# A four-layer transformer issued in turns, in the order of its source

## The chip, the cores and the metric

The kernel runs on one core of one Trainium2 chip. The metric is the device time of one execution in microseconds. A core has five engines with a queue each: TensorE (PE, with its weight loads shown apart as PEld), VectorE (DVE), ScalarE (ACT), GpSimd (POOL) and SyncE (SP), which here issues the DMAs. Each engine takes its instructions in the order in which they stand in its queue, and waits where one needs a result of another engine.

## The reference

A tensor of 16 sequences of 256 tokens with 128 features goes through eight blocks, each added to the residual stream after a layer norm on either side. The third block, the one that is touched here, is itself a transformer of four layers:

```python
for i in range(DEPTH):      # 4
    x = x + self_attention(layer_norm(x, ln1_g[i], ln1_b[i]), Wq[i], Wk[i], Wv[i], Wo[i], bo[i])
    h = layer_norm(x, ln2_g[i], ln2_b[i])
    x = x + (jax.nn.gelu(h @ W1[i] + b1[i], approximate=False) @ W2[i] + b2[i])
```

Its self-attention has eight heads of 16. Four are local: windows of 128 tokens, where a query sees its own window up to itself and the window before it. Four are linear: a softmax over the features of q, elu(k) + 1, and a context per 64 tokens that is summed over the earlier ones. The MLP is 128 to 512 to 128 with a Gelu. All numbers are float32.

## The kernel before

The 16 sequences are handled as eight groups (`NG`) of two sequences, 512 tokens each, in four tiles of 128 tokens (`NT`). The whole program is one stage after another; each stage has its own pools of SBUF and PSUM. `stage_l1_attn` (L761) is the stage of the four-layer transformer. Its input is `z[g]`, the normed residual stream of group g, and it keeps the stream of the four layers in `z[g]`.

A group's layer has two generators. `l1_mix` (L832) is the attention: norm and transposes (`l1_norm_T`, L806), the products for Q and K (L848, L852), a product for the token-major rest (L864) with maxima and copies on DVE and ACT, then for each of two sequences the scores of the local heads with a mask added by a product (L883 to L890) and their row maxima on DVE (L891). The maxima are transposed onto Q (`q2T`, L905), the scores are computed a second time transposed (L933, L935), exponentiated on ACT (L938), cut to the causal part on POOL (L941), and multiplied with the values (L950, L952) into one PSUM tile with the tag `o`. The linear heads' context (L920) and products (L960) run beside. Two rounds of transposes (L975, L981) lead to the output product (L985), which DVE adds to `z` (L986). `l1_ffn` (L815) is the MLP: norm and transposes, four first products with a Gelu each (L824), the second products (`tokens_ps`, L338) into one PSUM tile, and an add on DVE (L829). A statistic of a norm is four instructions L255 and four L257 on DVE, then L244 and L245 on POOL; the norm itself is four L264 on DVE.

PSUM has eight banks. In this stage seven of them are one ring for the tags `s`, `mm` and `t`, and one is `o` (`RING_BANKS`, L37). All products go through the helper at L336, all transposes of a norm through L325, so the profile names products by their tiles. A float32 product appears as two passes in the profile: two MATMUL and two LDWEIGHTS.

What sets the order: the stage is traced by `interleave` (L219), which advances up to five generators at a time, one `yield` each in a round. The list has, for every layer, eight mixes and then eight MLPs. But the stage isn't in a manual schedule, so this is no more than a preference: the planner of the tile framework orders the instructions of each engine by its own costs and by what it takes to be ready. Other stages (`stage_l0`, the attentions, the last one) stand in `k.tc.manual_schedule()`, where every engine has its instructions in the order in which the source traces them, by the helper `turns`:

```python
def turns(self, items):
    now = 0
    items = [[start, 0, steps] for start, steps in items]
    while items:
        for item in items[:]:
            for _ in range(min(3, now - item[0] + 1 - item[1])):
                item[1] += 1
                if next(item[2], self) is self:
                    items.remove(item)
                    break
        now += 1
```

In each turn every item that has started takes one step, from one `yield` to the next, in the order of the list. `idle(n)` is n empty steps.

The stage before (`stage_l0`) leaves the last group's first MLP output, `y7`, unfinished; `rest_of_l0` (L752) norms and adds it beside the first mix. In the last layer `ffn` (L782) also norms and adds the result to `x[g]` for groups 0 to 5, and `then` (`fill`, L994) stores `x[g]` and norms it for the next stage. Groups 6 and 7 (`k.over`) leave that to the next stage, which can't start before this one has given back its pools.

Of the kernel before, what the change touches and what calls it, by code (L numbers as in the profile page):

```python
# [750 lines left out]

def rest_of_l0(k, x, z, y):  # L752

    yield from k.residual(x, y)
    yield
    nb, rs = k.stats_nb(x)
    yield
    k.normed_act(z, x, nb, rs)


def stage_l1_attn(k, x, ws, rows, z, then, xn, y7, xT0):  # L761


    nc = k.nc

    k.l1_val = [k.t([P, NT, 4, 32], f"l1_val{i}", 1) for i in range(3)]
    k.l1_lin = [k.t([P, NT, 65], f"l1_lin{i}", 1) for i in range(3)]
    k.l1_ctx = [k.t([P, 4, 68], f"l1_ctx{i}", 1) for i in range(2)]  # L770
    k.l1_max = [k.t([P, 2, 3, 4, 32], f"l1_max{i}", 1) for i in range(2)]
    for a in k.l1_val + k.l1_lin:
        nc.vector.memset(a, 1.0)
    for a in k.l1_max + k.l1_ctx:
        nc.gpsimd.memset(a, 0.0)
    for a in k.l1_ctx:
        nc.gpsimd.tensor_copy(a[:, :, 64:68], bc(k.c["head16"], 1, 4))
    k.cb = {n: k.t([P, P], "b_" + n, 1, dt=BF16) for n in ("ident", "negmask")}
    for n, a in k.cb.items():
        nc.vector.tensor_copy(a, k.c[n])  # L780

    def ffn(i, g):  # L782
        late = i == 3 and g in k.over
        yield from l1_ffn(k, z[g], ws[i], rows[f"b2{i}"], xn[g] if late else z[g])
        if i == 3 and not late:
            yield
            yield from k.residual(x[g], z[g])
            yield
            yield from then(g)

    steps, leads = [], []
    for i in range(4):
        steps += [l1_mix(k, z[g], ws[i], rows[f"bo{i}"], NG * i + g, xT0 if i + g == 0 else None) for g in range(NG)]
        steps += [ffn(i, g) for g in range(NG)]
        leads += [4] * NG + [2] * NG

    def beside(a, b):
        for _ in a:
            next(b, k)
            yield  # L800

    steps[0] = beside(steps[0], rest_of_l0(k, x[NG - 1], z[NG - 1], y7))
    k.interleave(steps, 5, leads, -1)


def l1_norm_T(k, z, g, b):  # L806

    xn = yield from k.norm(z, "xn")
    ps = k.transposed_ps(xn)
    out = k.t([P, GT], "xT", 2)  # L810
    k.nc.scalar.activation(out, ps, AF.Identity, bias=b, scale=g)
    return out


def l1_ffn(k, z, w, b2, out):  # L815

    hT = yield from l1_norm_T(k, z, w["ln2_g"], w["ln2_b"])
    k.nc.gpsimd.tensor_tensor(z, z, bc(b2, 1, NT), ALU.add)
    yield
    h = k.t([P, 4, GT], "mlp_h", 3)  # L820
    for f in range(4):
        ps = k.ps("s")
        k.mm(ps, w["w1"][:, f * P : (f + 1) * P], hT)
        k.nc.scalar.activation(h[:, f, :], ps, AF.Gelu, bias=w["b1"][:, f : f + 1])  # L824
        if f % 2:
            yield
    ps = k.tokens_ps(h, w["w2"].rearrange("p (c n) -> p c n", c=4))
    yield
    k.nc.vector.tensor_tensor(out, ps, z, ALU.add)  # L829


def l1_mix(k, z, w, bo, n, hT=None):  # L832
# [6 lines left out]
    heads = [slice(32 * h, 32 * h + 32) for h in range(4)]  # L839
    tiles = lambda b: [slice((2 * b + t) * P, (2 * b + t + 1) * P) for t in range(2)]  # L840
    if hT is None:
        hT = yield from l1_norm_T(k, z, w["ln1_g"], w["ln1_b"])
    nc.gpsimd.tensor_tensor(z, z, bc(bo, 1, NT), ALU.add)
    yield

# [6 lines left out]
    k.mm(ps, w["wk"], hT)  # L852
    kT = k.t([P, GT], "kT", 3)
    nc.scalar.activation(kT, ps, AF.Identity, bias=k.c["one16"])

    q = k.t([P, 2, 2, 64], "q", 2)
    kr = k.t([P, NT, 64], "kr", 2)
# [2 lines left out]
    for half in range(2):  # L860
# [10 lines left out]
        nc.scalar.activation(ke[:, ts, :], ps[:, :, 64:128], AF.Exp)  # L871
        nc.scalar.copy(val[:, ts, :, 0:16], ps[:, :, 128:192].rearrange("p t (h d) -> p t h d", d=16))
        nc.scalar.copy(lin[:, ts, 0:64], ps[:, :, 192:256])
    yield

# [3 lines left out]
    for b in range(2):  # L879
        (q0, q1), both = tiles(b), slice(2 * b * P, (2 * b + 2) * P)  # L880
        ss = [k.ps("s") for _ in heads]
        for r, s in zip(heads, ss, strict=True):
            k.mm(s[:, 0:P], qT[r, q0], kT[r, q0], True, False)  # L883
        for r, s in zip(heads, ss, strict=True):
            k.mm(s[:, P : 3 * P], qT[r, q1], kT[r, both], False, False)


        for h, s in enumerate(ss):
            s = s[:, : 3 * P].rearrange("p (j n) -> p j n", j=3)
            k.mm(s[:, 0:3:2, :], ident, bc(negmask, 1, 2), False, True)  # L890
            v.tensor_reduce(mx[:, b, :, h, 16], s, AX.X, ALU.max, negate=True)  # L891
        v.tensor_tensor(mx[:, b, 1, :, 16], mx[:, b, 1, :, 16], mx[:, b, 2, :, 16], ALU.min)
        if b == 0:


            nc.scalar.activation(q, q, AF.Exp)
            v.scalar_tensor_tensor(ke, ke, 1.0, kr, ALU.min, ALU.add)
        yield
    q2T = k.t([P, GT], "q2T", 2)
    tp = k.ps("mm")  # L900
    for b in range(2):
        for t in range(2):
            at = mx[:, b, t].rearrange("p h n -> p (h n)")
            nc.tensor.transpose(tp[:, (2 * b + t) * P : (2 * b + t + 1) * P], at, k.c["ident"])
    v.tensor_tensor(q2T, tp, qT, ALU.add)  # L905

    halves = [slice(0, 64), slice(64, P)]
    tp = k.ps("mm")
# [1 line left out]
        nc.tensor.transpose(tp[:, t * P : (t + 1) * P], q[:, t].rearrange("p b n -> p (b n)"), k.c["ident"])  # L910
    linT = k.t([P, SEQ], "linT", 2)
    nc.scalar.copy(linT, tp[:, :SEQ])

    cps = k.ps("mm")[:, : 3 * 65].rearrange("p (u n) -> p u n", u=3)
    first = slice(0, 64)
# [13 lines left out]
    for b in range(2):  # L929
        (q0, q1), both = tiles(b), slice(2 * b * P, (2 * b + 2) * P)  # L930
        ss = [k.ps("s") for _ in heads]
        for r, s in zip(heads, ss, strict=True):
            k.mm(s[:, 0:SEQ], kT[r, q0], q2T[r, both], True, False)  # L933
        for r, s in zip(heads, ss, strict=True):
            k.mm(s[:, SEQ : 3 * P], kT[r, q1], q2T[r, q1], False, True)  # L935
        e = k.t([P, 4, 3, P], "e", 3)
        for h, s in enumerate(ss):
            nc.scalar.activation(e[:, h].rearrange("p j n -> p (j n)"), s[:, : 3 * P], AF.Exp)  # L938
# [50 lines left out]
def soft_inputs(k, x, pool):  # L989
# [1 line left out]
    xs = k.dram.tile([P, NG, NT, D], F32, tag="xs", name="xs")  # L991
    xn = [pool.tile([P, NT, D], F32, tag=f"mxn{g}", name=f"mxn{g}") for g in range(NG)]

    def fill(g):  # L994
        k.nc.sync.dma_start(out=xs[:, g], in_=x[g])
        nb, rs = k.stats_nb(x[g])
        yield
        k.normed_act(xn[g], x[g], nb, rs)

    return xs, xn, fill  # L1000
# [1067 lines left out]
```

## Time and profile before

| | |
|---|---|
| median of 3 runs | 2963.91 us (2961.12 to 2964.82) |
| profiled execution, its own time | 2960.44 us |
| its span, from the first to the last instruction | 2958.7 us |
| mean granted TensorE clock | 0.968 of full |
| PE busy | 2757.9 us, 93% of the span |
| DVE, ACT, POOL busy | 1931.3, 1676.9, 1017.2 us |
| the changed stage | from 175.0 to 948.45 us |

The profile shows one execution. A group of instructions is given by source line, engine, operation and tiles (written, then read), with a count, the busy time and the mean length; after a bar stand the idle time of the engine ahead of them and who ended it. A timeline line gives start, length, engine, line, operation, tiles, shape and count, and in brackets the idle time before it and what released it. The ends of matmuls are modelled and they overlap in the pipeline, so a stretch of TensorE is best read from start to start.

### The profile page before, as it was taken

What the parts mean: (1) busy time and instruction counts of PE and PEld (TensorE: products, weight loads), DVE (VectorE), ACT (ScalarE), POOL (GpSimd) and SP (SyncE); (2) the same over time, 40 slices, a digit from 0 to 9 for tenths busy, and PEclk for the clock granted to TensorE, in tenths of its full rate; (3) what the DMA queues carried; (4) which work ended last, traced back from release to release, by engine and by line L of the source; (5) the groups of instructions that cost most, each with busy time, mean ns of one, the idle gap of its engine ahead of it and who ended that gap; (6) DMA issues with size and microseconds to landing.
All of it is one profiled execution on the core that took longest, in us unless ns stands there. A gap on an engine that the chain in (4) does not pass through costs nothing.

```text
span 2958.7 us, 59454 instructions
## 1 busy us (share of the span) xinstructions
PE 2757.9 (93%) x23674; PEld 1878.8 (63%) x23674; DVE 1931.3 (65%) x5302; ACT 1676.9 (57%) x3530; POOL 1017.2 (34%) x1407
## 2 busy tenths in 40 slices
PE   8989999999998799999988998799999799978998
PEld 4556776777766588888863443566666444436897
DVE  5677466565666889999967765666574587735442
ACT  6745656455465676777735666444434377756543
POOL 3553333333336200000044555423221466644332
PEclk9989999999999899999988999899999899998999
DMA  4000000000001000000020000000000000010000
GB/s 116 12 1 2 1 2 2 1 2 1 2 2 38 1 12 12 8 9 8 9 71 5 1 1 1 1 1 1 1 1 1 1 1 1 1 51 7 2 16 16
DMA packets 29150, 31.30 MB, mean 11 GB/s; under 512 B 7292, under 2 KB 20156, under 8 KB 28732
## 3 DMA queue, kind: packets, MB, share of 16 engines
q1 hardware_dynamic: 28872, 27.49, 3.1%
q8 instruction: 187, 3.06, 0.4%
q14 instruction: 91, 0.75, 0.1%
HBM read 23.29 MB, written 4.19 MB: 9 GB/s over the span
## 4 chain that ended last, share of the span: by engine, by line
PE 50%; ACT 7%; DVE 7%; POOL 2%; issue 2%; DMA 0%; POOLq 0%; SPq 0%; ACTq 0%; DVEq 0%
PE ps_s L336 31%; PE ps_o L336 7%; PE ps_mm L336 6%; ACT at_e L491 1%; PE ps_s L325 1%; ACT lg L1199 1%; PE ps_xin L336 1%; ACT meT L1206 1%; PE ps_sum L336 1%; ACT mdisp L1106 1%; ACT lg L1079 1%; PE ps_t L1204 1%; DVE at_nm L459 1%; PE ps_s L525 1%; DVE scan L1488 1%
## 5 line engine op out<-in xcount | busy, mean ns | idle before, releaser
L459 DVE TENSOR_REDUCE at_nm<-ps_s 128x2 f32<-128x512 f32 (+1 forms) x384 | 238.1, 682 | 119.7 <-PE ps_s L336 119.7
L491 ACT ACTIVATE at_e<-ps_s 128x512 f32<-128x512 f32 x384 | 198.2, 603 | 96.7 <-PE ps_s L336 94.6
L1488 DVE TENSOR_TENSOR scan<-ps_s,lm 128x384 f32<-128x384 f32 x256 | 124.7, 549 | 142.4 <-PE ps_s L336 142.2
L497 POOL TENSOR_SCALAR_AFFINE_SELECT at_e<-at_e 128x1024 f32<-128x1024 f32 (+1 forms) x96 | 135.1, 1408 | 208.1 <-ACT at_e L491 207.8
L245 POOL TENSOR_TENSOR ln_rs<-ln_rs,mhalf 128x4 f32<-128x4 f32 x192 | 196.6, 1024 | 15.2
L1015 POOL TENSOR_TENSOR ln_rs<-ln_mv,mendt 128x4 f32<-128x4 f32 x6 | 1.2, 199 | 521.2 <-DVE ln_mv L1013 521.2
L891 DVE TENSOR_REDUCE l_max<-ps_s 128x3 f32<-128x384 f32 x256 | 124.1, 548 | 61.5 <-PE ps_s L336 61.5
L336 PE MATMUL ps_o<-my,meT 128*128 128x129 f32 x1024 | 144.1, 288 | 20.8 <-ACT mgot L1218 16.5
L336 PEld LDWEIGHTS ps_s<-l_w,mlp_h 128*128 128x128 f32 x1280 | 149.7, 192 | 20.3 <-issue 15.1
L336 PE MATMUL ps_s<-l1f_phi,mxT 128*128 128x256 f32 x512 | 141.8, 401 | 21.5 <-DVE mpart L1080 15.7
L244 POOL TENSOR_SCALAR ln_rs<-ln_mv 128x4 f32<-128x4 f32 x184 | 38.5, 209 | 338.0 <-DVE ln_mv L257 317.3
L336 PEld LDWEIGHTS ps_o<-my,meT 128*128 128x128 f32 x1024 | 127.8, 195 | 39.3 <-ACT mgot L1218 22.2
L336 PE MATMUL ps_s<-l_w,mlp_h 128*128 128x128 f32 x1280 | 151.0, 275 | 1.3 <-ACT mlp_h L824 0.9
L336 PE MATMUL ps_s<-qm,kT 32*128 32x512 f32 x768 | 144.4, 650 | 8.0 <-DVE at_nm L459 7.8
L336 PE MATMUL ps_s<-km,qT 32*128 32x512 f32 x768 | 138.4, 666 | 8.7 <-DVE qT L1632 3.7
L941 POOL TENSOR_SCALAR_AFFINE_SELECT e<-e 128x512 f32<-128x512 f32 x128 | 78.6, 635 | 172.8 <-ACT e L938 172.8
L336 PE MATMUL ps_o<-at_e,at_vm 128*32 128x128 f32 (+1 forms) x2048 | 122.7, 336 | 15.3 <-ACT at_oT L521 15.3
L336 PE MATMUL ps_mm<-mdisp,mxn 128*128 128x128 f32 x1024 | 125.3, 279 | 5.0 <-DVE mdisp L1118 4.9
L938 ACT ACTIVATE e<-ps_s 128x384 f32<-128x384 f32 x256 | 105.4, 510 | 39.4 <-PE ps_s L336 39.4
L1465 ACT COPY BT<-ps_s 128x512 f32<-128x512 f32 x64 | 37.6, 587 | 158.0 <-PE ps_s L336 158.0
L336 PEld LDWEIGHTS ps_mm<-mdisp,mxn 128*128 128x128 f32 x1024 | 121.8, 195 | 7.9 <-DVE mdisp L1118 6.6
L336 PEld LDWEIGHTS <-b_ident 128*128 128x128 bf16 x656 | 51.9, 99 | 113.1 <-issue 102.5
(462 smaller groups left out, 7203.1 us busy)
## 6 DMA issues: line engine op xcount, KB each, us to landing
mw<-in_l1fw SPq DMA_DIRECT2D x16, 256.0 KB, 2.6
moe_w<-in_moe SPq DMA_DIRECT2D x16, 256.0 KB, 5.4
l_w<-in_l SPq DMA_DIRECT2D x10, 256.0 KB, 3.3
x<-in_x SPq DMA_DIRECT2D x8, 256.0 KB, 5.8
xs<-x SPq DMA_DIRECT2D x8, 256.0 KB, 2.1
out<-x SPq DMA_DIRECT2D x8, 256.0 KB, 2.5
slT<-xs SPq DMA_DIRECT2D x6, 256.0 KB, 2.7
l1f_phi<-in_l1f SPq DMA_DIRECT2D x1, 1024.0 KB, 5.0
```

Source lines behind the costliest of these rows:

```text
L244: g.tensor_scalar(out, in_, scale, eps, ALU.mult, ALU.add)
L245: g.tensor_tensor(out, out, self.mhalf[:, :n], ALU.pow)
L325: self.nc.tensor.transpose(out[:n, k * P : (k + 1) * P], src[:, k, cols], self.c["ident"])
L336: self.nc.tensor.matmul(out, lhsT=lhsT, rhs=rhs, start=start, stop=stop, skip_group_check=True)
L459: v_.tensor_reduce(nm[:, t, r, vs], s, AX.X, ALU.max, negate=True)
L491: nc.scalar.activation(e[:, r], s, AF.Exp)
L497: nc.gpsimd.affine_select(at, at, [[0, 4], [0, n], [1, P]], ALU.is_ge, 0.0, base=0, channel_multiplier=-1)
L891: v.tensor_reduce(mx[:, b, :, h, 16], s, AX.X, ALU.max, negate=True)
L938: nc.scalar.activation(e[:, h].rearrange("p j n -> p (j n)"), s[:, : 3 * P], AF.Exp)
L941: nc.gpsimd.affine_select(e[:, :, j, :], e[:, :, j, :], [[0, 4], [1, P]], ALU.is_ge, 0.0, base=0, channel_multiplier=-1)
L1465: nc.scalar.copy(s, ps)
L1488: v.tensor_tensor(m, s[:, : SEQ + P], lm[:, SCAN_HEADS[4 * (t // 2) + 2 * i + hh], :], ALU.mult)
```

## The change

The stage gets a manual schedule. Each mix and each MLP is an item of `turns`. Mix n (layer n // 8, group n % 8) has its transposes in turn `at[n]`: 0, 5, 11, 16, 22 and from then on every eight turns. Its norm begins six turns earlier, its last step is 16 turns later, and the MLP of the same group and layer begins 17 turns after `at[n]`. The items stand in the list by falling start, so within a turn the item that started last comes first. `rest_of_l0` is the last item and starts at turn 0.

For this the steps are cut anew. A mix has yields between Q, K and the first half of the values, between the halves, two after the first sequence's scores, one after Q's exponential, one ahead of the linear context, an empty one between the sequences' second scores, one between the two weighted sums and one behind their copy. Norms wait 5 steps in a mix, 3 in an MLP, and there is one more step between a norm and its transposes. The exponential of `q` stands behind both sequences' scores instead of the first's, the sum for `ke` behind `q2T`.

Two things change in the work itself. The masks are the first product into each score tile instead of the last; the maxima then follow the scores directly. And an MLP's second products go into the `o` tile instead of one of the ring, in three parts (tile 0; tiles 1 and 2; tile 3) with a step each. `mlp_h` has two buffers instead of three. The numbers computed are the same.

```diff
 def rest_of_l0(k, x, z, y):
-    yield from k.residual(x, y)
+    yield from k.residual(x, y, 3)
     yield
     nb, rs = k.stats_nb(x)
-    yield
+    yield from idle(3)
     k.normed_act(z, x, nb, rs)
...
         if i == 3 and not late:
             yield
-            yield from k.residual(x[g], z[g])
+            yield from k.residual(x[g], z[g], 3)
             yield
-            yield from then(g)
-    steps, leads = [], []
-    for i in range(4):
-        steps += [l1_mix(k, z[g], ws[i], rows[f"bo{i}"], NG * i + g, xT0 if i + g == 0 else None) for g in range(NG)]
-        steps += [ffn(i, g) for g in range(NG)]
-        leads += [4] * NG + [2] * NG
...
-    steps[0] = beside(steps[0], rest_of_l0(k, x[NG - 1], z[NG - 1], y7))
-    k.interleave(steps, 5, leads, -1)
+            yield from then(g, 3)
+    at = [0, 5, 11, 16, 22] + [32 + 8 * n for n in range(4 * NG - 5)]
+    items = []
+    for n, start in enumerate(at):
+        i, g = divmod(n, NG)
+        items.append((start - (0 if n == 0 else 6), l1_mix(k, z[g], ws[i], rows[f"bo{i}"], n, xT0 if n == 0 else None)))
+        items.append((start + 17, ffn(i, g)))
+    items = sorted(items, key=lambda item: -item[0])
+    with k.tc.manual_schedule():
+        k.turns(items + [(0, rest_of_l0(k, x[NG - 1], z[NG - 1], y7))])
-def l1_norm_T(k, z, g, b):
-    xn = yield from k.norm(z, "xn")
+def l1_norm_T(k, z, g, b, wait):
+    xn = yield from k.norm(z, "xn", 2, wait)
+    yield
     ps = k.transposed_ps(xn)
...
 def l1_ffn(k, z, w, b2, out):
-    hT = yield from l1_norm_T(k, z, w["ln2_g"], w["ln2_b"])
+    hT = yield from l1_norm_T(k, z, w["ln2_g"], w["ln2_b"], 3)
...
-    h = k.t([P, 4, GT], "mlp_h", 3)
+    h = k.t([P, 4, GT], "mlp_h", 2)
...
-    ps = k.tokens_ps(h, w["w2"].rearrange("p (c n) -> p c n", c=4))
-    yield
+    ps = k.ps("o").rearrange("p (t d) -> p t d", t=NT)
+    w2 = w["w2"].rearrange("p (c n) -> p c n", c=4)
+    for t in range(NT):
+        for f in range(4):
+            k.mm(ps[:, t, :], h[:, f, t * P : (t + 1) * P], w2[:, f, :], f == 0, f == 3)
+        if t in (0, 2):
+            yield
     k.nc.vector.tensor_tensor(out, ps, z, ALU.add)
...
-        hT = yield from l1_norm_T(k, z, w["ln1_g"], w["ln1_b"])
+        hT = yield from l1_norm_T(k, z, w["ln1_g"], w["ln1_b"], 5)
...
     nc.scalar.activation(kT, ps, AF.Identity, bias=k.c["one16"])
+    yield
...
         nc.scalar.copy(lin[:, ts, 0:64], ps[:, :, 192:256])
-    yield
+        if half == 0:
+            yield
...
         ss = [k.ps("s") for _ in heads]
+        for s in ss:
+            k.mm(s[:, : 3 * P].rearrange("p (j n) -> p j n", j=3)[:, 0:3:2, :], ident, bc(negmask, 1, 2), True, False)
         for r, s in zip(heads, ss, strict=True):
-            k.mm(s[:, 0:P], qT[r, q0], kT[r, q0], True, False)
+            k.mm(s[:, 0:P], qT[r, q0], kT[r, q0], False, False)
         for r, s in zip(heads, ss, strict=True):
-            k.mm(s[:, P : 3 * P], qT[r, q1], kT[r, both], False, False)
+            k.mm(s[:, P : 3 * P], qT[r, q1], kT[r, both], False, True)
         for h, s in enumerate(ss):
             s = s[:, : 3 * P].rearrange("p (j n) -> p j n", j=3)
-            k.mm(s[:, 0:3:2, :], ident, bc(negmask, 1, 2), False, True)
             v.tensor_reduce(mx[:, b, :, h, 16], s, AX.X, ALU.max, negate=True)
         v.tensor_tensor(mx[:, b, 1, :, 16], mx[:, b, 1, :, 16], mx[:, b, 2, :, 16], ALU.min)
         if b == 0:
-            nc.scalar.activation(q, q, AF.Exp)
-            v.scalar_tensor_tensor(ke, ke, 1.0, kr, ALU.min, ALU.add)
-        yield
+            yield
+            yield
+    nc.scalar.activation(q, q, AF.Exp)
+    yield
...
     v.tensor_tensor(q2T, tp, qT, ALU.add)
+    v.scalar_tensor_tensor(ke, ke, 1.0, kr, ALU.min, ALU.add)
...
     nc.scalar.copy(linT, tp[:, :SEQ])
+    yield
...
         es.append(e)
         yield
+        if b == 0:
+            yield
...
+        if b == 0:
+            yield
     oT = k.t([P, GT], "oT", 1)
     nc.scalar.copy(oT, o)
+    yield
...
-    def fill(g):
+    def fill(g, wait=1):
         k.nc.sync.dma_start(out=xs[:, g], in_=x[g])
         nb, rs = k.stats_nb(x[g])
-        yield
+        yield from idle(wait)
         k.normed_act(xn[g], x[g], nb, rs)
```

More of the change, by code (lines that the diff above doesn't have):

```diff
@@ L786, in ffn @@
             yield
-            yield from k.residual(x[g], z[g])
+            yield from k.residual(x[g], z[g], 3)
             yield
-            yield from then(g)
-    steps, leads = [], []
-    for i in range(4):
-        steps += [l1_mix(k, z[g], ws[i], rows[f"bo{i}"], NG * i + g, xT0 if i + g == 0 else None) for g in range(NG)]
-        steps += [ffn(i, g) for g in range(NG)]
-        leads += [4] * NG + [2] * NG
-    def beside(a, b):
-        for _ in a:
-            next(b, k)
-            yield
-    steps[0] = beside(steps[0], rest_of_l0(k, x[NG - 1], z[NG - 1], y7))
-    k.interleave(steps, 5, leads, -1)
-def l1_norm_T(k, z, g, b):
-    xn = yield from k.norm(z, "xn")
+            yield from then(g, 3)
[11 more added lines that the diff above has]
+    yield
     ps = k.transposed_ps(xn)
@@ L992, in soft_inputs @@
     xn = [pool.tile([P, NT, D], F32, tag=f"mxn{g}", name=f"mxn{g}") for g in range(NG)]
-    def fill(g):
+    def fill(g, wait=1):
         k.nc.sync.dma_start(out=xs[:, g], in_=x[g])
         nb, rs = k.stats_nb(x[g])
-        yield
+        yield from idle(wait)
         k.normed_act(xn[g], x[g], nb, rs)
```

## The prediction

> **What bounds the kernel now.** I read the page first, then the table of stretches over the stage that the change touches, then the timeline of one steady group in it. The page:
>
> ```profile
> PE 2757.9 (93%) x23674; PEld 1878.8 (63%) x23674; DVE 1931.3 (65%) x5302; ACT 1676.9 (57%) x3530; POOL 1017.2 (34%) x1407
> PEclk9989999999999899999988999899999899998999
> ```
>
> TensorE is busy nearly everywhere, so the changed stage can only gain what it now loses between its own products. That stage begins with the product into `ps_s` from `hand_xT` at 175.0 us and ends with the last DVE add of an MLP at 948.45: 773.5 us. In stretches (columns: stretch, its length, busy us of PE, PEld, DVE, ACT, POOL with instructions, granted clock, DMA share, GB/s):
>
> ```profile
> 175.00:226.00 51.00, 43.77 (x333) 28.53 (x333) 37.51 (x163) 23.40 (x64) 26.41 (x44) 0.80 0.00 1
> 376.00:565.00 189.00, 185.84 (x1747) 133.23 (x1746) 112.26 (x413) 103.81 (x231) 63.76 (x89) 1.00 0.01 1
> 905.00:949.00 44.00, 41.19 (x252) 30.86 (x251) 26.04 (x136) 25.15 (x48) 27.87 (x47) 1.00 0.08 31
> ```
>
> A layer in the middle is 98% PE-busy; only the start has idle PE and a clock of 0.80. But matmuls overlap, so busy is not full. The timeline of one mix shows what is lost inside (start, length, engine, line, operation, count, idle before):
>
> ```profile
> 419.57 1.02 PE L336 MATMUL ps_s<-xT,l_wq 128*128 128x512 f32 x2
> ...
> 424.56 0.68 PE L336 MATMUL ps_s<-kT,qT 32*128 32x128 f32 x4
> 425.44 1.30 PE L336 MATMUL ps_s<-kT,qT 32*128 32x128 f32 x12 [0.21 <-ACT e L938]
> 426.68 0.61 PE L336 MATMUL ps_s<-b_negmask,b_ident 128*128 128x256 bf16 x4
> 427.22 1.31 PE L336 MATMUL ps_s<-q2T,kT 32*128 32x256 f32 x16
> 428.45 1.16 PE L336 MATMUL ps_s<-l_wo,catT 128*128 128x128 f32 x8
> 429.54 0.94 PE L336 MATMUL ps_s<-kT,qT 32*128 32x128 f32 x16
> 430.41 0.61 PE L336 MATMUL ps_s<-b_negmask,b_ident 128*128 128x256 bf16 x4
> ...
> 435.50 1.02 PE L336 MATMUL ps_s<-xT,l_wq 128*128 128x512 f32 x2
> ```
>
> Mixes repeat every 15.93 us (419.57 to 435.50). The same 16 score products take 0.87 us to the next start when nothing holds them (429.54 to 430.41) and 2.12 us when they wait for PSUM that ACT still reads (424.56 to 426.68): 1.25 lost. The 16 products from `q2T` take 0.87 (423.11 to 423.98) or 1.23: 0.36 lost. With about 0.2 of small gaps a mix has 14.15 us of work and 1.8 of waiting. MLPs have their own stretch at 7.45 us each (adds L829 that far apart), which is their work alone. So 14.15 + 7.45 = **21.6 us of PE work per group and layer, 691 for 32**; 82 of the 773.5 are lost. The Q copies of layers 1 and 2 begin at 376.62 and 565.20: 188.6 per layer, 15.8 over 8 x 21.6. The first layer (from 177.27) takes 199.4, 10.8 more: the start.
>
> **What the skill says.** *TensorEngine Tiling (Array Packing)*, Key Properties: changing the tiling mode drains TensorE. The trace agrees: four masks start 0.11 apart, but the 32-row or 32-column products behind them come 0.09 later than that. *ScalarE: Activation LUTs*, What ACT_TABLE_LOAD costs: 1283 ns, plus a drain of about 1380. Here each load takes 1283 and the next ACTIVATE can start 0.01 us later, so I use 1.28. *PSUM — Partial Sum Buffer*, The four PSUM rules: a first product clears the written-bits of its whole bank, so a later one without that flag overwrites columns the first left out. This lets a mask over blocks 0 and 2 go first; no time follows from it, and no trace here tests it. *TensorE: Matmul & The Clock Gate*, Part 1: idle of about a 3.4 us window halves the clock. At 185 to 195 us the granted clock is 0.50, after PE waits of 2.41 and 2.06.
>
> **The change, part by part.** (1) The order. Before, the planner ordered the stage: eight mixes, then eight MLPs. Now each engine issues in source order: a mix starts every eight turns and the MLP of an earlier group runs inside it; in a turn the item started last goes first. The same 21.6 us of PE work fall in eight turns. With turn r counted from the transposes of mix n, they are: r0 its transposes, third of an earlier MLP, scores from `q2T` of n-1, output product of n-2; r1 Q and K, two thirds; r2 first values, last third, second scores of n-1; r3 second values, masks, scores; r3 and r4 weighted sums of n-1; r5 transposes of MLP n-2, masks, scores, linear part of n-1; r6 and r7 the MLP's first products between the small transposes.
>
> The waits, from durations of the rows. In r3 values (0.86), masks (0.53 with the mode change) and scores (0.94 to the last end) put the first maximum at 2.37 us after the turn's start. Four L891 take 1.95 (427.00), the minimum 0.17. Behind them on DVE, in r4, stand the four L264 of MLP n-2, 1.12. Its transposes head PE's r5 and end 0.15 after:
>
> ```profile
> 427.00 1.95 DVE L891 TENSOR_REDUCE l_max<-ps_s 128x3 f32<-128x384 f32 x4 [2.17 <-PE ps_s L336]
> 908.71 1.12 DVE L264 TENSOR_SCALAR xn<-z,ln_mv,ln_rs 128x128 f32<-128x128 f32 x4 [1.71 <-POOL ln_rs L245]
> 909.50 0.60 PE L325 MATMUL ps_s<-const_ident,xn 128*128 128x128 f32 x4
> ```
>
> 2.37 + 1.95 + 0.17 + 1.12 + 0.15 = 5.75. PE without a wait would leave those transposes at 0.86 + 0.53 + 0.87 + 1.44 + 0.44 = 4.15. So PE stands for **1.5 us in each period**, everything in r5 behind it. Next late would be the maxima of r5: last score ends 1.4 after the masks start, DVE is done 2.2 later; linear part 0.4, two first products 1.72 and the first two transposes 0.22 cover it to within 0.1. A period is 21.6 + 1.5 = 23.1 against 188.6 / 8 = 23.6. About 28 periods have the pair: 42 us.
>
> (2) Masks first: the same 256 masks by 0.11. They wait for the PSUM bank alone and the maxima begin 0.2 sooner after the scores; counted above. (3) MLP outputs in three parts in the `o` bank: the same 1,024 products at 112 ns. The bank is free: the sum's copy L954 ends in r4, the MLP's add at the end of r2, 2.3 us before the next sum. That takes one tile off the ring of seven. Eight turns now take 34 ring tiles, so a bank comes back after 1.6 turns, 4.8 us, and the ring's waits of 1.6 per mix go; the tightest is the last score tile of r3, which follows the second exponential of r2's scores by 0.1. On POOL the select behind those scores (L941, 1.23) ends 0.1 after r4's sum could start: hidden in the 1.5. (4) Activation tables: Exp and Gelu now alternate, two loads per group, 64 for the stage's 24:
>
> ```profile
> L824 ACT ACT_TABLE_LOAD x12 | 15.4, 1283 | 0.2
> L938 ACT ACT_TABLE_LOAD x8 | 10.3, 1283 | 0.9 <-PE ps_s L336 0.8
> ```
>
> 40 x 1.28 = 51 us more on ACT, which has 424 busy of 774. Nothing on PE: the Gelu load runs while PE does r5's scores, the Exp load while it does the MLP's third; uncovered, they would be 2.57 per group. (5) Longer norm waits, `mlp_h` at two buffers, `ke` and `q` later: nothing, a group has 32 turns between its MLP's end and its next norm. (6) Last layer: six residuals put a statistic (1.23) into r3 ahead of r4's L264, and a norm into r6: 1.2 per group, **7 us**; DMAs `xs<-x` go out earlier on SP, which has nothing else then. (7) The start: mix 0 alone, its maxima and group 7's norm ahead of the norm of mix 1, so PE stands about 6 us after 181 and goes cold. By turn 16, some 46 us in, I count 31.5 us of work: **15 lost**, where before 20 were lost by 226. (8) The end: the last group's sums, then its MLP with nothing beside it: exp and select before the sum (2.4), statistics to normed (2), copy (1), last Gelu (0.8), add (0.8): **7**.
>
> Sum: 691 + 42 + 7 + 15 + 7 = 762, against 773.5: -11.5. Made on the profiled execution's 2960.4 (span 2958.7 and 1.7 around it) this gives 2948.9; the median of the runs is 3.5 higher, so **2952**.
>
> **Rivals.** *The DVE wait does not arise* (PE finds its transposes ready): the 42 go, 2910. For it: DVE is busy only 60% of a layer. Against: it is a matter of order, not load. *Slower: DVE paces r3 to r6.* If the maxima of r5 are not covered either, or normed rows take the 0.34 to 0.56 each they take under POOL's work, the wait grows. Everything else saves 773.5 - 720 = 53, over 28 periods 1.9 us: past that the change loses. At 2.6 us it is 28 x 1.1 = 31 more than mine, 20 slower: 2984. *Nothing:* many small semaphore waits of 0.05 to 0.1, which a source order meets and a planner had placed around, eat the gain: +0.4 per group, 2964.
>
> **How the numbers follow.** Faster as worked out 46%, its own range 2938 to 2957; no DVE wait 14%; nothing 15%; slower 25%. Past 0.2% (6 us, about what a measurement here can tell) faster is 0.60, same 0.15, slower 0.25. The wait's bounds, 0 to 2.6 us, give 2910 to 2984; leaving out half of the first rival and the far tail of the last, 2924 to 2984.
>
> **What would show it.** Right: PE idle before L325 named DVE `xn` L264, about 1.5 us a group; Q copies 8 turns and 23.1 us apart; some 64 table loads in the stage with no PE wait behind; no waits of scores on ACT `e`; L891 starting after scores, not masks. Wrong: periods of 24 or more; PE waiting for `mlp_h` L824 after a load; PE cold past 220 us; or a later stage ordered otherwise by the planner, which would move time outside 175 to 949.

## The result, and the profile after

The changed kernel takes 2976.49 us (median of 4 runs, 2974.32 to 2977.19) against 2962.51 for the kernel before on the same chip: a ratio of 1.0048, 95% interval 1.0035 to 1.0061. It is slower by some 14 us. The forecast was 2952, faster, with 2938 to 2957 as the range of its own mechanism. The measured time lies outside that one and inside the whole range of 2924 to 2984. The profiled execution has a span of 2974.7 us against 2958.7.

The page of the changed kernel, its busy times and granted clock:

```profile
PE 2738.7 (92%) x23674; PEld 1857.6 (62%) x23674; DVE 1935.3 (65%) x5302; ACT 1726.7 (58%) x3570; POOL 1015.9 (34%) x1407
PEclk9989999999999899999988999899999899998999
```

The work of PE and DVE is what it was. ACT does 49.8 us more, in 40 more instructions. PE is busy for 19 us less while the span is 16 us longer, so it stands for longer. The stage now runs from 174.61 us to the end of the last MLP's add at 963.99: 789.4 us against 773.5. That is the whole of the 16 us; no other stage moved.

The stretches of the changed kernel (stretch, its length, busy us of PE, PEld, DVE, ACT, POOL with instructions, granted clock, DMA share, GB/s):

```profile
175.00:226.00 51.00, 39.62 (x316) 24.25 (x314) 32.20 (x125) 23.13 (x64) 17.32 (x30) 0.78 0.00 1
226.00:365.00 139.00, 130.41 (x1243) 89.84 (x1243) 81.41 (x284) 84.25 (x169) 44.83 (x62) 0.99 0.01 1
376.00:565.00 189.00, 179.92 (x1781) 128.01 (x1778) 113.64 (x414) 118.27 (x244) 63.29 (x89) 1.00 0.01 1
807.00:910.00 103.00, 94.32 (x872) 65.63 (x871) 69.56 (x282) 62.97 (x133) 47.00 (x72) 0.95 0.03 12
```

In the middle, 376 to 565, PE does 1781 products where the kernel before did 1747 in the same time: this part is faster, although PE is busy for 179.92 us and not for 185.84. The times between mixes say the same: in the middle the Q copies (the instruction on ACT that writes a mix's `qT`) come 23.27 us apart, so eight groups take 186.2 us where a layer took 188.6. Busy time is no measure of the gain here. The other three stretches are the start, the time up to the ninth mix, and the last layer; they turn out to matter more.

The timeline of one period in the middle, around r4 and r5:

```profile
510.47 0.94 PE L336 MATMUL ps_s<-kT,qT 32*128 32x128 f32 x16
511.34 1.51 PE L336 MATMUL ps_o<-e,l_val 128*32 128x256 f32 x32
511.43 1.95 DVE L899 TENSOR_REDUCE l_max<-ps_s 128x3 f32<-128x384 f32 x4 [0.67 <-PE ps_s L336]
513.41 0.17 DVE L900 TENSOR_TENSOR l_max<-l_max 128x4 f32<-128x4 f32 x1
513.50 1.11 DVE L264 TENSOR_SCALAR xn<-z,ln_mv,ln_rs 128x128 f32<-128x128 f32 x4
513.98 1.00 PE L325 MATMUL ps_s<-const_ident,xn 128*128 128x128 f32 x4 [1.14 <-DVE xn L264]
514.83 0.60 PE L336 MATMUL ps_s<-b_negmask,b_ident 128*128 128x256 bf16 x4
```

This is the queue on DVE that the prediction described: four maxima, a minimum, the four normed rows of an MLP, and PE standing in front of the transposes for 1.14 us. The transposes then follow the rows one by one, 0.85 us to the masks. The waits of PE over 18 such periods (388 to 807 us; total, times, longest) have one entry, and nothing waits for `e` or for a table:

```profile
PE ps_s L325 <- DVE xn L264: 20.4, 18, 1.1
```

### The profile page after: what moved, and what is told of

Its sections match the earlier page's. It is cut to its first block, busy times and chain, and to the rows that moved or that the text cites. A ratio compares the mean times of both kernels' runs of the same rounds, so it can differ in the third digit from the quotient of the medians.

```text
span 2974.7 us, 59582 instructions
## 1 busy us (share of the span) xinstructions
PE 2738.7 (92%) x23674; PEld 1857.6 (62%) x23674; DVE 1935.3 (65%) x5302; ACT 1726.7 (58%) x3570; POOL 1015.9 (34%) x1407
## 4 chain that ended last, share of the span: by engine, by line
PE 76%; DVE 10%; ACT 9%; POOL 2%; issue 2%; DMA 0%; SPq 0%; POOLq 0%; ACTq 0%; DVEq 0%
PE ps_s L336 50%; PE ps_o L336 11%; PE ps_mm L336 6%; PE ps_s L325 4%; DVE l_max L899 2%; ACT at_e L491 1%; ACT lg L1215 1%; PE ps_xin L336 1%; ACT meT L1222 1%; PE ps_sum L336 1%; ACT mdisp L1122 1%; ACT lg L1095 1%; DVE ln_st L255 1%; PE ps_t L1220 1%; PE ps_s L525 1%
## 5 line engine op out<-in xcount | busy, mean ns | idle before, releaser
L336 PEld LDWEIGHTS ps_o<-l_w,mlp_h 128*128 128x128 f32 x1024 | 126.0, 192 | 19.6 <-issue 12.4
L336 PE MATMUL ps_o<-l_w,mlp_h 128*128 128x128 f32 x1024 | 130.2, 276 | 4.6 <-ACT oT L969 4.5
L336 PE MATMUL ps_s<-xT,l_w 128*128 128x512 f32 x256 | 126.8, 619 | 1.3 <-ACT xT L811 1.3
L336 PEld LDWEIGHTS <-b_ident 128*128 128x128 bf16 x656 | 58.7, 102 | 103.5 <-issue 86.6
```

The source lines that it names most:

```text
L336: self.nc.tensor.matmul(out, lhsT=lhsT, rhs=rhs, start=start, stop=stop, skip_group_check=True)
```

## The experiments

To compare runs I cut the stage at the 32 Q copies, one for each mix: start to the ninth copy, 19 periods to the 28th, four periods of the last layer to the 32nd, and the end. Under source order a mix and its neighbours stand at the same point at each copy, so these cuts compare kernels with the same pattern of eight turns. For the kernel before only the sum can be compared. The start of the same code differs by up to 2 us between runs (189.8 to 191.9); smaller differences there are not read. "Ratio to before" compares runs on the same chip.

```
                         start   19 periods (each)   last 4    end    stage    time      ratio to before
before                                                                773.5    2962.5
changed                  190.4   442.2 (23.27)       102.9     53.9   789.4    2976.5    1.0048
rows early               190.2   412.6 (21.72)        89.7     49.8   742.3    2929.9    0.9895
Relu for Gelu            189.8   442.2 (23.28)       103.7     53.9   789.6    2971.8    1.0047
outputs in the ring      190.5   446.3 (23.49)       101.8     53.4   792.1    2982.9    1.0077
masks last               191.3   440.7 (23.19)        99.4     53.8   785.1    2972.0    1.0033
residual later           191.9   442.2 (23.27)        97.5     60.6   792.3    2981.2    1.0071
no residual              191.9   442.2 (23.27)        92.2     52.5   778.8    2964.5    1.0012
even starts alone        180.2   442.3 (23.28)       102.8     53.6   778.9    2967.1    1.0011
rows early, even starts  170.2   412.7 (21.72)        89.6     51.5   724.0    2910.4    0.9830
```

One flaw of this division: from the 30th mix on, the copy starts 0.87 us sooner behind its product than before (in the Relu run it does so throughout). So in every row but Relu "last 4" reads 0.87 too low and "end" as much too high; differences between those rows stand. Counted from the products, the last four periods of the change are 26.22, 26.32, 24.85 and 26.33 us, 103.7 in all.

### The normed rows one turn earlier

```diff
-    xn = yield from k.norm(z, "xn", 2, wait)
-    yield
+    xn = yield from k.norm(z, "xn", 2, wait)
+    yield from idle(1 + more)
...
-    hT = yield from l1_norm_T(k, z, w["ln2_g"], w["ln2_b"], 3)
+    hT = yield from l1_norm_T(k, z, w["ln2_g"], w["ln2_b"], 2, 1)
```

> The MLP's normed rows (L264) are issued one turn earlier, in r3 ahead of the four maxima, and its transposes stay in r5. Theory (the wait in r5 is a matter of the order on DVE): the idle before L325 named DVE xn, 1.14 us in each of 18 periods after the change, goes, and the Q copies come 22.0 us apart instead of 23.27 because the maxima of r5 then set a small wait before the transposes of the maxima. 24 periods by 1.27 is 30: about 2946. Rival (DVE paces r3 to r6): the same time is lost before the transposes of the maxima instead, the Q copies stay 23.0 to 23.3 apart, and the time stays within 5 us of 2976.

Measured: 2929.85 us, ratio 0.9895 (0.9879 to 0.9912), 47 us below the change, where 30 were expected. The timeline of a period of this run, around its r3 to r5:

```profile
499.31 1.10 DVE L264 TENSOR_SCALAR xn<-z,ln_mv,ln_rs 128x128 f32<-128x128 f32 x4
...
501.84 1.95 DVE L899 TENSOR_REDUCE l_max<-ps_s 128x3 f32<-128x384 f32 x4 [0.67 <-PE ps_s L336]
503.19 0.66 PE L325 MATMUL ps_s<-const_ident,xn 128*128 128x128 f32 x4
503.68 0.60 PE L336 MATMUL ps_s<-b_negmask,b_ident 128*128 128x256 bf16 x4
```

And the stretch of the middle in this run, with the columns as above:

```profile
376.00:565.00 189.00, 189.00 (x1867) 137.47 (x1866) 121.09 (x449) 125.02 (x260) 68.17 (x96) 1.00 0.01 2
```

The rows are done before the maxima start, the transposes take 0.49 us and have no wait. PE is busy throughout and a period is 21.72 us. So the wait cost 1.55 us a period: 1.14 of standing and 0.36 in transposes that followed the rows one by one (0.85 instead of 0.49) are most of it. The same DVE work, ahead of the maxima in its queue instead of behind them, costs nothing. My theory held in its mechanism; the rest of the wait that I had left for the next maxima is not there, and the last layer and the end gained too. The rival, that DVE paces these turns, falls.

### Activation tables

```diff
-        k.nc.scalar.activation(h[:, f, :], ps, AF.Gelu, bias=w["b1"][:, f : f + 1])
+        k.nc.scalar.activation(h[:, f, :], ps, AF.Relu, bias=w["b1"][:, f : f + 1])
```

> The MLPs of this stage use Relu in place of Gelu, which leaves Gelu out of the computation and with it the alternation of activation tables. Theory (the 64 table loads are hidden on ACT): the loads of the stage go, and the time stays within 4 us of 2976. Rival (part of the 82 us of loads stands on PE's path): at least 10 us go.

This run leaves the Gelu out, so its numbers are others; it is read for its time alone. Measured: 2971.78 us, ratio 1.0047 (1.0031 to 1.0063), against the change's 1.0048. The time is 4.7 us below the change's, a little past the 4 of my theory, but on a chip where the kernel before was 2.4 faster too. The stage has one load instead of 64, and its length is 789.6 against 789.4. The groups of the changed kernel in this stage show what was taken away (busy us, mean ns, idle before):

```profile
L824 ACT ACT_TABLE_LOAD x32 | 41.1, 1283 | 0.6
L949 ACT ACT_TABLE_LOAD x27 | 34.6, 1283 | 25.5 <-PE ps_s L336 25.4
```

So 82 us of loads on an engine that waits anyway were free, as forecast.

### The outputs back in the ring

```diff
-    ps = k.ps("o").rearrange("p (t d) -> p t d", t=NT)
+    ps = k.ps("mm").rearrange("p (t d) -> p t d", t=NT)
```

> All MLP outputs back in a tile of the ring of seven, in the same three parts and the same order. Theory (the order of turns, not the bank, sets the period): the Q copies stay within 0.2 of 23.27, and the start gets back the 4.5 us in which PE waited for the o bank (ACT oT, three times): 2972. Rival (the ring is short without the bank): waits of PE for ring tiles come back, periods of 24.0 and more, 2990 or later.

Measured: 2982.94 us, ratio 1.0077 (1.0062 to 1.0092), between the two times expected. The period grows by 0.22, a little over what my theory allowed, and far less than the rival's 0.7. The `o` bank is thus worth 4 us in the 19 periods; the order of turns removed the old waits for the ring, not the bank: between 388 and 777 us PE waits here for nothing but `xn`. The start gained nothing: the waits for `oT` went, but another of 1.9 us, for `l_lin` (a copy on ACT for the linear heads), came.

### Masks last

```diff
-        for s in ss:
-            k.mm(s[:, : 3 * P].rearrange("p (j n) -> p j n", j=3)[:, 0:3:2, :], ident, bc(negmask, 1, 2), True, False)
...
+            k.mm(s[:, 0:3:2, :], ident, bc(negmask, 1, 2), False, True)
             v.tensor_reduce(mx[:, b, :, h, 16], s, AX.X, ALU.max, negate=True)
```

On the changed kernel:

> The changed kernel with the masks as the last products of the scores again, each followed by its maximum. Theory (masks first are worth nothing by themselves): the first maximum of r3 starts within 0.3 us of where it does now, the Q copies stay within 0.2 of 23.27, and the time within 5 us of 2976. Rival (masks first hold the maxima back, which now wait for all scores): periods of 23.0 or less, 2970 or earlier.

Measured: 2972.01 us, ratio 1.0033 (1.0023 to 1.0043), periods of 23.19. The same edit on the kernel with early rows:

> The MLP's rows one turn earlier (2929.9), with the masks last again. Theory (masks last gave 0.08 a period because the maxima, and with them the rows behind, came sooner; with the rows ahead nothing waits for them): Q copies stay at 21.72, within 3 us of 2930. Rival (masks first cost PE itself, by the changes of tiling mode): periods of 21.6 or less and 2926 or earlier.

Measured: 2931.45 us, ratio 0.9896 (0.9882 to 0.9911), periods of 21.94 us. Both times lie where the two first theories put them, but neither theory had what the periods show: masks last are 0.08 better a period where PE waits for the maxima's queue, and 0.22 worse where PE is the bound. By the order of the products, masks last make two more changes of tiling mode for each mix (from scores back to masks, twice). *TensorEngine Tiling (Array Packing)*, Key Properties, in the Trainium skill says that such a change drains TensorE, and this run agrees: ahead of the scores the values take 1.06 us (497.02 to 498.08) where with early rows and masks first they take 0.97 to the masks, and ahead of the second scores the transposes take 0.59 (500.94 to 501.53) where they took 0.49. Masks that go first follow the values in the same mode. Both sizes are small beside the rest.

### The residual of the last layer

First moved by two turns, then left out.

```diff
         if i == 3 and not late:
-            yield
+            yield from idle(3)
             yield from k.residual(x[g], z[g], 3)
```

> In the last layer the residual of six groups starts two turns later, so that its statistic (1.23 us of DVE) stands in r5 and not in r3 behind the maxima and ahead of L264. Theory (the last layer's periods of 24.9 to 26.3 us, against 23.27, come from that statistic): they fall to 23.3 to 24, and about 8 us go: 2968. Rival (they come from the transfers to DRAM or from the clock of 0.97 that these periods show): no change, 2976.

Measured: 2981.21 us, ratio 1.0071 (1.0056 to 1.0086): later, not earlier. The last four periods give 5.4 us back, less than expected. But the end takes 60.6 instead of 53.9, since the residual and the normed rows of the next stage now fall between the last MLPs: PE waits twice, 4.6 us in all, for the copy `xT` on ACT, which stands behind four such rows (1.65 us) both times. What was saved in the last layer was paid at the end.

```diff
-            yield from k.residual(x[g], z[g], 3)
+            yield from idle(3)
```

> The changed kernel without the residual of six groups in the last layer (its statistic, rows and addition are left out, its turns kept; the next stage's copy and normed rows stay). Theory (the residual's DVE work, 1.23 in r3 and 1.12 in r6, makes the last layer's periods of 24.9 to 26.3 us): they fall to 23.3 to 23.6, and 8 to 10 us go: 2967. Rival (the other half of that work, the copy to DRAM with its statistic in r7 and four ACT rows, is what delays): periods of 24.5 and more, 2972 or later.

Without the residual the output is another one; again only the time is read. Measured: 2964.45 us, ratio 1.0012 (1.0004 to 1.0021), 12 us below the change; the stage is 10.6 shorter. Counted from the products, the last four periods are 23.27 like all others. So it is the residual that makes the last layer slow; the copy to DRAM and its statistic, which stayed, do not. The timeline of the changed kernel in this layer, at the second of these periods' waits, shows how:

```profile
840.20 1.95 DVE L899 TENSOR_REDUCE l_max<-ps_s 128x3 f32<-128x384 f32 x4 [0.67 <-PE ps_s L336]
...
842.27 0.86 DVE L255 BATCH_NORM_STATS2 ln_st<-z 128x6 f32<-128x128 f32 x4
...
843.33 1.08 DVE L264 TENSOR_SCALAR xn<-z,ln_mv,ln_rs 128x128 f32<-128x128 f32 x4
...
843.79 1.00 PE L325 MATMUL ps_s<-const_ident,xn 128*128 128x128 f32 x4 [2.17 <-DVE xn L264]
...
845.16 1.46 PE L336 MATMUL ps_s<-kT,qT 32*128 32x128 f32 x16
...
846.55 0.73 PE L336 MATMUL ps_s<-l_ctx,linT 64*64 64x68 f32 x16
...
847.22 2.78 PE L336 MATMUL ps_s<-xT,l_w 128*128 128x512 f32 x4
```

The statistic stands where the prediction put it, and the wait grows from 1.14 to 2.17. Then come two things that it had priced at nothing. After the longer wait the scores take 1.46 instead of 0.94, the linear products 0.73 instead of 0.47 and the MLP's first four 2.78 instead of 1.98. The clock around the first wait, which ends at 817.6:

```profile
816.00:819.00 3.00, 1.43 (x7) 0.86 0.00 0
819.00:822.00 3.00, 3.00 (x36) 0.58 0.00 0
822.00:825.00 3.00, 3.00 (x15) 1.00 0.00 0
```

That makes a period another 1.5 us longer, in three of the four; the one of 24.85 us has the same wait of 2.17 and no loss of clock, and so has a fifth such wait, at the end (921.3). The other thing is a second queue on DVE. In r6 the residual's own four rows (1.11 us) stand ahead of the next mix's rows, so the transposes of that mix start later behind those of `cat` (0.63 instead of 0.50) and follow their rows one by one, 0.84 us to the next product instead of 0.43. The first line is from a period in the middle, the second from the last layer:

```profile
522.75 0.60 PE L325 MATMUL ps_s<-const_ident,xn 128*128 128x128 f32 x4
879.01 1.01 PE L325 MATMUL ps_s<-const_ident,xn 128*128 128x128 f32 x4
```

That is 0.5 us more, in all four periods.

### The starts

The changed kernel starts its first mixes at turns 0, 5, 11, 16, 22, 32 and every eighth from there. Most of the runs here alter this on the kernel with early rows, the last but one on the changed kernel:

```diff
-    at = [0, 5, 11, 16, 22] + [32 + 8 * n for n in range(4 * NG - 5)]
+    at = [0, 5, 10, 15, 20] + [30 + 8 * n for n in range(4 * NG - 5)]
```

> On top of the MLP's rows one turn earlier (2929.9), the first mixes start at turns 0, 5, 10, 15, 20, 30 in place of 0, 5, 11, 16, 22, 32, then every eight as before. No mix is then 11 to 14 turns behind another, which is where an MLP's output parts meet the weighted sums in the one o bank. Theory (the start loses 4.5 us to that bank between 250 and 298 us): these waits on ACT oT go, 2925. Rival (the start is held by the latency of the first mixes and by the cold clock, whatever the bank does): within 2 us of 2930.

Measured: 2935.39 us, ratio 0.9908 (0.9892 to 0.9925). Neither theory had this: the waits for `oT` went, but the start takes 195.3 us instead of 190.2: PE waits 10 us there for normed rows, up to 3.6 at once.

```diff
+    at = [5 * n for n in range(NG)] + [45 + 8 * n for n in range(3 * NG)]
```

> As the run with fives, but all eight mixes of the first layer start five turns apart (0 to 35), the ninth at 45, then every eight. Theory (between 220 and 380 us PE lacks products because too few items are under way: 19 us lost there): a good half of it comes back, 2918. Rival (in denser turns the maxima of two mixes and the ring of seven meet, and PE waits for them instead): 2928 or later.

Measured: 2948.99 us, ratio 0.9952 (0.9937 to 0.9967). The denser start is the slower one: 200.7 us to the ninth copy, with copies up to 26.9 us apart while five turns lie between mixes, and the 19 periods behind it take 421.8 instead of 412.6, since the last of these mixes are still out of step with those that follow. Too little under way was not the trouble, and my theory fell. Giving the first three MLPs a tile of the ring instead of the `o` bank helps little:

```diff
+        yield from l1_ffn(k, z[g], ws[i], rows[f"b2{i}"], xn[g] if late else z[g], "mm" if NG * i + g < 3 else "o")
```

> The MLP's rows one turn earlier (2929.9), with the outputs of the first three MLPs in tiles of the ring. Theory (three waits of 4.5 us in all for the o bank are a true part of the start's loss): 2 to 4 us go, 2926 to 2928. Rival (PE then waits for something else in the same turns): 2929 to 2932.

Measured: 2928.59 us, ratio 0.9889 (0.9874 to 0.9904); the interval can't tell it from 0.9895. The trace puts 3.0 us less at the start, part of them lost again at the end.

```diff
+    at = [8 * n for n in range(4 * NG)]
```

> The MLP's rows one turn earlier (2929.9), with all mixes eight turns apart from the first on, in place of 0, 5, 11, 16, 22, 32. Theory (the start loses because few items are under way, whatever their spacing): wider is worse at first, PE idles through eight turns of one mix: 2935 or later. Rival (denser starts were later in two runs, so the spacing itself costs, through DVE's queue and the o bank): 2926 or earlier.

Measured: 2910.36 us, ratio 0.9830 (0.9814 to 0.9847). My theory fell and the rival held, by more than it said: the start takes 170.2 us instead of 190.2, though it has eight turns more. The same stretch, before the ninth mix, in this run:

```profile
226.00:365.00 139.00, 139.00 (x1382) 100.72 (x1381) 88.38 (x324) 92.38 (x190) 48.93 (x68) 1.00 0.01 2
```

1382 products against 1243 in the changed kernel, and no wait of PE. The pattern of eight turns is what keeps each wait covered; a mix that is five, six or ten turns from the next puts transposes beside maxima, and an MLP's outputs beside the sums in the `o` bank. It is not one wait. In the changed kernel PE stands in this stretch for these (total, times, longest):

```profile
PE ps_o L336 <- ACT oT L969: 4.5, 3, 2.7
PE ps_s L325 <- DVE xn L264: 2.0, 3, 1.1
PE ps_s L325 <- DVE cat L993: 0.9, 1, 0.9
```

and just ahead of it for 2.4 us on `cat` at 222.8, after which the clock is 0.74 from 225 to 230. With the starts alone altered, on the changed kernel:

> The changed kernel with nothing but the starts altered: all mixes eight turns apart. Theory (the uneven starts put mixes and MLPs out of the order that the eight turns were made for, and that alone cost the change its sign): by 380 us some 18 to 22 us less are lost, and later periods stay at 23.27: 2957, level with the kernel before or faster by up to 0.3%. Rival (even starts give so much only where the rows come early): 2968 or later, still slower than before.

Measured: 2967.11 us, ratio 1.0011 (1.0004 to 1.0017), nearer to the rival. The start takes 180.2 us, 10.2 less than in the change. The other 10 of the 20 go to the DVE wait, which even starts meet from the fourth mix on: six times and 6.8 us between 226 and 365, where the change has three and 2.0. So uneven starts cost the change 10 us, of the 16 by which its stage is longer than the one before.

These 10 us are not all waits. From the start to the ninth copy, first the change and then the run with even starts alone (columns as above):

```profile
174.61:365.04 190.43, 170.46 (x1558) 114.43 (x1559) 113.64 (x409) 107.41 (x231) 62.46 (x94) 0.94 0.01 1
174.82:354.98 180.16, 163.16 (x1558) 112.43 (x1559) 109.25 (x409) 105.51 (x229) 62.40 (x94) 0.95 0.01 1
```

Both do the same 1558 products. PE stands for 20.0 us in the one and 17.0 in the other, which is 3 of the 10. The other 7.3 are products that take longer. Part of that is the clock: with uneven starts it is 0.72 from 205 to 215 us and 0.87 from 225 to 235, where even starts have 1.00; they have the lower one from 195 to 205 (0.72 against 0.84). Weighted with PE's busy time, the stretches from 175 to 235 lose some 3 us more, by my estimate.

```diff
+    at = [0] + [3 + 8 * n for n in range(4 * NG - 1)]
```

> Rows early and starts eight apart (2910.4), but the second mix three turns behind the first, and the others eight apart from there: five turns fewer, one pair out of step. Theory (what costs is being out of step over many turns; two mixes side by side cover each other's waits at first): 2 to 5 us go, 2906 to 2908. Rival (any pair out of step costs more than the turns saved): 2911 or later.

Measured: 2918.54 us, ratio 0.9849 (0.9836 to 0.9863). My theory fell again: one pair out of step costs more than the five turns that it saves, and the start takes 177.5 us instead of 170.2.

### The end

Two runs tried to fill the end, the first on the kernel with early rows, the second with even starts too:

```diff
-        items.append((start + 17, ffn(i, g)))
+        items.append((start + (23 if n == 4 * NG - 2 else 17), ffn(i, g)))
```

> On top of the MLP's rows one turn earlier (2929.9), the last MLP but one starts six turns later, with its output in a tile of the ring, so that its products stand between those of the last MLP. Theory (the end loses the last MLP's chain: 1.1 before its transposes, 0.9 before its first products, and products at half the clock): 4 us go, 2926. Rival (the chain of the last group sets the end, and what stands beside it only delays it): 2930 or later.

Measured: 2936.11 us, ratio 0.9907 (0.9893 to 0.9922). The products that now stand between the last MLP's had covered the last mix: PE waits there for `cat` 1.80, `catT` 0.73 and the last rows 2.29, and the clock over the last 44 us is 0.88.

```diff
+    at = [8 * n for n in range(4 * NG - 1)] + [8 * (4 * NG - 2) + 3]
```

> Rows early and starts eight apart (2910.4), but the last mix three turns behind the one before, so that the last two mixes and MLPs run side by side. Theory (the end loses 8 to 10 us to the chain of the last group, with half the clock after its waits): 4 us go, 2906. Rival (the pair waits for the maxima and the o bank instead): 2911 or later.

Measured: 2917.19 us, ratio 0.9843 (0.9828 to 0.9858). The stage is 2.3 us longer than with all mixes eight apart, and the next one begins with slower products (3.65 us for its first eight, against 1.97). Both rivals held by the time. The waits that the second one named are small, though: behind 800 us PE waits 1.0 us for maxima and 0.2 for the sums' copy `oT`. I have nothing that shortens the end. The fastest kernel of the study is the one with early rows and even starts, 1.7% below the kernel before.

## Why the prediction was wrong

The sum was 691 + 71 = 762 for the stage; it is 789.4. Set out over the same cuts, with 32 x 21.72 = 695.0 as work (the period of the run in which PE never stood):

```
                                   forecast                           measured
work                               691                                695.0
the DVE wait, 19 periods           19 x 1.5 = 28.5                    442.2 - 19 x 21.72 = 29.5
last layer, 4 periods              4 x (1.5 + 1.2) = 10.8             103.7 - 4 x 21.72 = 16.8
start and end, 9 mixes             15 + 7 + 5 x 1.5 + 2.2 = 31.7      the rest, 48.1
```

(The forecast has 28 waits of 1.5 us, 23 of them in the two rows above the last and five in it, and 7 us for six residuals, of which four are in the third row.)

**Steps (1) to (5) held.** The wait sits in r5 in front of L325, named DVE `xn`, behind four maxima, a minimum and four rows; it is 1.55 us against 1.5 (the prediction's own terms give 1.6: 5.75 less 4.15). PE's work of a group and layer is 21.72 against 21.6, the Q copies are 23.27 apart against 23.1. The stage has 64 table loads, none of which costs anything. The first rival, that the wait does not arise, and the one in which many small semaphore waits eat the gain, are both excluded by these periods. The slower rival gave the right sign by the wrong mechanism: at 1.55 the wait is under the 1.9 from which it decides. That the time lies in the whole range is therefore luck: its slow side was made for a wait of up to 2.6 us, which did not come.

**Step (7), the start, failed.** "By turn 16, some 46 us in, I count 31.5 us of work: 15 lost", and from there the sum took the steady period as given. To see what was lost I price every product with its mean time to the next start in the steady periods of the run with early rows, kind by kind, so that a period's products sum to 21.72 us; the losses that follow are estimates from this. Turn 16 begins at 224.2 us, 49.6 us in, with 27.9 us of work done: 21.7 are lost, not 15. PE stands for 11.8 us up to there, where the step spoke of about 6. From turn 16 to the ninth mix another 16.2 are lost, where at most the five waits of 1.5, 7.5 in all, were counted. Starts 5, 6, 5, 6 and 10 turns apart were priced as if they gave the same pattern as starts eight apart; they are in none of the step's terms. So the start loses 37.9 us against 22.5, and with even starts alone 27.6. The sign that I named as one of those for a wrong forecast, PE cold past 220 us, was there: 0.74 at 225 to 230, after the wait of 2.4 us.

**Step (6), the last layer, was mis-sized.** The statistic is where it was put, and delays the rows by about what it takes: the wait grows by 1.03. Per period 1.2 was taken; 2.7 were measured (103.7 less four periods of 23.27, by four). The residual's rows in r6, which the step named, cost 0.5 of their own, and the lower clock behind the wait 1.5 in three periods of four. The step put the clock at nothing, although the prediction had shown 0.50 behind a wait of 2.41 us. Without the residual the stage is 10.6 us shorter, where 7 were counted.

**Step (8), the end, was about right.** By the same pricing it loses 10.6 us behind the last Q, where 7 and the 2.2 of two residuals were counted; with rows early and even starts it is 8.2.

So of 27 us, 16 lie in the start and end, nearly all of them in the start, 6 in the last layer, 4 in the work of a period and 1 in the wait. Neither of the first two turns the sign alone: even starts alone are at 1.0011 and no residual at 1.0012, both still slower than before by their intervals, if by little.

What stays open is how the loss of the start divides. Of the 10 us that even starts save, 3 are standing and some 3 the clock; the rest of the longer products I can't name. With early rows the `o` bank alone is about 3, and another uneven spacing brings other waits.

## What to carry to other kernels

When an order is written as a pattern of turns, price the turns before it is even as a case of their own: list them with their real offsets, since every cover that was reckoned for the pattern may be missing there. Here the pattern at its own spacing from the first item on was faster than each denser start that was run. When an engine with slack makes the bound engine wait, move the instructions that are late ahead in its queue before anything else; here 1.1 us of rows, ahead of the maxima instead of behind them, gave 47 us. And a wait that becomes longer is not priced by its length alone: look at the clock of the products behind it.

## What the runs showed of the hardware that I had not expected

- A wait of 2.17 us was followed by a lower TensorE clock in three of five cases (0.58 in the next 3 us after the first one), while one of 1.14 us in 18 periods never was (1.00 throughout). The length alone does not decide: after the same wait of 2.68 us for `oT`, ahead of the same products, the clock from 299 to 302 us is 1.00 in the changed kernel and 0.54 in the run with early rows, and in the latter two waits of 0.59 and 0.90 us close together (up to 238.5 and 241.3) were followed by 0.56 from 242 to 245. *TensorE: Matmul & The Clock Gate*, Part 1, in the Trainium skill gives an idle window of about 3.4 us, running freely, so that the point varies; here less than that was enough.
- The place of the masks in a bank's products has a price of either sign: 0.22 us a period for two changes of tiling mode when PE is the bound, and 0.08 the other way when the maxima's queue is.
- Table loads of 1283 ns, 64 of them on an engine with idle time, changed the length of the stage by 0.2 us when they were taken out.
